# A three-stage transformer layer on one core: the twice folded filter's common part in three pieces from the sixth phase on, early weight transfers held back, first norms in another order

## The chip, the cores and the metric

The kernel runs on one core of a Trainium2 chip. The core has a matrix engine (PE; its weight loads are listed apart as PEld), a vector engine (DVE), a scalar or activation engine (ACT), a general engine (POOL) and a queue engine (SP) that issues most DMAs. The metric is the device time of one launch in microseconds (us). Smaller is better.

## The reference

The input is a 2 x 1024 x 512 float32 tensor. Four blocks follow each other, each a residual on the normalised input: differential attention with a filter along the tokens, a mixture of 8 experts of which 2 are kept, a linear attention with rotary embedding, and the same mixture again. The change touches the first block only:

```python
q, k, v = (norm(x) @ W for W in (Wq, Wk, Wv))      # 16 heads, two halves of 16 each
q, k = rotary(q), rotary(k)                        # interleaved pairs
attn1, attn2 = causal(q1, k1, v), causal(q2, k2, v)
f = rfft(attn1, axis=1) - lambda_full * rfft(attn2, axis=1)
attn = irfft(f * exp(-0.5 * (linspace(0, 1, n) / 0.15) ** 2), n=1024, axis=1)
attn = attn * rsqrt(mean(attn * attn, -1) + eps) * rms_weight * (1 - LAMBDA_INIT)
x = x + attn.reshape(2, 1024, 512) @ Wout
```

The filter in frequency is a circular convolution along the 1024 tokens. The kernel does it with 128 x 128 blocks of taps.

## The kernel before

**Opening.** The first batch's eight tiles of 128 tokens are loaded in the order 4, 5, 6, 7, 0, 1, 2, 3 and normalised in pairs. `pair_sums` (DVE statistics, then two ACT functions for the inverse root) and `pair_scale` (three small DVE operations, then two 128x512 scalings, line 125) are called for one pair after another, each pair's sums ahead of the scaling of the pair before. `spread` turns a tile with four PE transposes (L313) and one ACT copy (L316). `project` makes 256 tokens of queries and keys of a unit with four matmuls that the trace counts as eight (L344); piece k-1 is called after the tiles of pair k are turned, and the last piece at the end. `project_values` (L368) makes the values. `rotate` multiplies the raw result and a copy of it with neighbouring rows exchanged (`other`, a DMA on SP, L360) by two tables and adds them (L388 to L390; DVE for unit 0, POOL for the others). It then sends parts to `keys` (L392, SP) and, once per unit, to `swapped` (L397: two DMAs from `qk`, two from `keys`). For unit 0 all four of those last DMAs are issued by ACT, for the other units by SP.

**Transfers.** DMAs on SP wait for each other only by place in the queue, by the data they need and by their buffers. A load of weights into a tile that nothing has used yet needs nothing. `load_others` brings the first expert weight `wdr`, `wup` and the filter's taps `filt`; `load_weights` and `load_values` bring 256 KB of attention weights for each later unit or pair of units.

**The attention loop.** There are 16 units (batch, quarter of the heads, half of a quarter) of nine phases. The loop counts steps t = 9 x unit + phase, from 0 to 143, and six more steps that drain it. One step makes the scores of two row blocks (L464, L477, PE), finds their minima (L491, L499, DVE), exponentiates (L508, ACT), joins the two halves of the step before (L543, DVE, with ratios from POOL, L528 and L536), transposes the joined weights of the step before that (L567, PE, and L569, ACT), and takes in whatever the dictionaries `small`, `large`, `middle`, `final` and `rear` list for that step. `large` entries share one PSUM bank per step while their widths add up to 512. `weigh` (L594) and `finish` (L616) turn weights into results at steps 9u+6, 9u+7, 9u+11 and 9u+13 (12 for the last two units). `fold` adds and subtracts rows of the result on POOL. PE, DVE, ACT and POOL keep the order in which the program calls; SP's order comes from a scheduler.

**Mixing.** The first four tiles of the second block's input (`MIXED`) are filtered inside the last two units, where unit 15 has no next unit to project. With t0 = 126 the first step of unit 14:

- `mix_common` (four matmuls of 256 columns, which the trace counts as eight, L719; an ACT copy, L728) at t0+5 for one half of the columns and t0+8 for the other; `mix_part` 0 and 1 (two POOL operations of 128x256 each, L748) one step later.
- `mix_apart` (four matmuls of 512 columns, L734; copy L739) at t0+9 and t0+10; `mix_part` 2 and 3 (two POOL operations of 128x512, L751 and L752) one step later.
- per tile n: `mix_square` (POOL, L756) at t0+10+n, `mix_sum` (DVE, L760) one step later, `mix_tables` (ACT) and `mix_scale` (three small DVE operations, then POOL, L771) after that; `mix_turn` (four transposes, L777, and a copy, L780) and `mix_project` (four matmuls of 512 columns, L786, and a DVE addition, L788) at t0+14, +17, +18 and +19, that is at steps 140, 143, 144 and 145. Steps from 144 on have no scores any more.
- POOL scales one quarter of `wout` (L851) in each of the steps 135 to 138.

The lines that set these places:

```python
            FILTER = [5, 8, 9, 10]
            TURN = [14, 17, 18, 19]
            t = (NU - 2) * NP
            for k, f in enumerate(FILTER):
                at(large, t + f, mix_common if k < 2 else mix_apart, 512, k % 2)
                at(middle, t + f + 1, mix_part, k)
```

## Time and profile before

| | |
|---|---|
| times of three runs | 1159.13, 1153.18 and 1149.43 us; median 1153.18 us |
| the profiled execution's own time | 1153.29 us |
| its span, first to last instruction | 1151.4 us, mean granted clock 0.988 |
| busy: ACT / POOL | 766.7 us (67%) / 437.8 us (38%) |
| first scores against `keys` (L477) | 38.02 us |
| steps 109 to 117 (unit 12, nothing mixed) | 40.28 us |
| steps 127 to 135 (unit 14) | 42.97 us |
| steps 136 to 143, to the last L534 | 47.75 us |
| from there to the end of the span | 439 us |

The steps are measured from one reciprocal of the join (L534, one in each step from 1 to 144) to the next. PE's work of a step starts up to 1 us ahead of that step's reciprocal. A row of the timeline gives start, duration, engine, line, operation, tiles and count, and in brackets how long the engine sat idle before and what released it. A row of the busy time by stretch gives the stretch, its length, the busy time of PE, PEld, DVE, ACT and POOL, the granted clock of the matrix engine, and the DMA share and rate.

### The profile page before, as it was taken

What the parts mean: (1) busy time and instruction counts of PE and PEld (TensorE: products, weight loads), DVE (VectorE), ACT (ScalarE), POOL (GpSimd) and SP (SyncE); (2) the same over time, 40 slices, a digit from 0 to 9 for tenths busy, and PEclk for the clock granted to TensorE, in tenths of its full rate; (3) what the DMA queues carried; (4) which work ended last, traced back from release to release, by engine and by line L of the source; (5) the groups of instructions that cost most, each with busy time, mean ns of one, the idle gap of its engine ahead of it and who ended that gap; (6) DMA issues with size and microseconds to landing.
All of it is one profiled execution on the core that took longest, in us unless ns stands there. A gap on an engine that the chain in (4) does not pass through costs nothing.

```text
span 1151.4 us, 23472 instructions
## 1 busy us (share of the span) xinstructions
PE 1068.3 (93%) x8680; PEld 732.3 (64%) x8680; DVE 930.3 (81%) x2034; ACT 766.7 (67%) x2009; POOL 437.8 (38%) x689
## 2 busy tenths in 40 slices
PE   6799999999889999999999888889999999998997
PEld 5677777777677787777777655545555544454554
DVE  5599999999889889989998987577777777757576
ACT  3488988989989889999989876243434333342533
POOL 0245456445354544634544562123232222223200
PEclk9999999999999999999999989899999999999999
DMA  5412211201301101110110611200000000000002
GB/s 194 156 47 66 59 35 57 61 27 45 116 16 38 45 17 36 46 43 15 39 43 20 235 55 39 110 1 1 1 1 1 1 1 0 1 1 37 1 19 92
DMA packets 33345, 52.19 MB, mean 45 GB/s; under 512 B 6480, under 2 KB 11088, under 8 KB 33104
## 3 DMA queue, kind: packets, MB, share of 16 engines
q1 hardware_dynamic: 32912, 50.17, 13.6%
q8 instruction: 69, 1.13, 0.4%
q10 hardware_dynamic: 320, 0.52, 0.2%
q14 instruction: 44, 0.36, 0.1%
HBM read 23.42 MB, written 6.29 MB: 26 GB/s over the span
## 4 chain that ended last, share of the span: by engine, by line
PE 54%; DVE 25%; ACT 12%; issue 5%; POOL 2%; DMA 2%; SPq 0%; DVEq 0%; POOLq 0%; ACTq 0%
DVE least L499 9%; ACT p L508 8%; PE s L477 7%; DVE p L543 6%; PE py L1269 4%; PE pq_q L1206 4%; PE pq_v L1206 4%; PE bank L344 4%; PE pq_k L1206 4%; PE dtp L567 4%; PE z L1010 3%; PE bank L594 3%; DVE least L491 3%; PE hr_f L1074 3%; PE po_f L1144 3%
## 5 line engine op out<-in xcount | busy, mean ns | idle before, releaser
L508 ACT ACTIVATE p<-s,least 128x640 f32<-128x640 f32 (+7 forms) x512 | 378.2, 744 | 47.5 <-DVE least L499 28.1
L499 DVE TENSOR_REDUCE least<-s 128x1 f32<-128x896 f32 (+5 forms) x384 | 244.2, 679 | 35.2 <-PE s L477 35.2
L543 DVE SCALAR_TENSOR_TENSOR p<-p,ratio,p 128x1024 f32<-128x1024 f32 (+7 forms) x256 | 226.7, 921 | 3.6 <-POOL ratio L536 3.4
L567 PE MATMUL dtp<-ident,p 128*128 128x128 f32 x1152 | 184.1, 283 | 11.8 <-ACT dt L569 7.6
L569 ACT COPY dt<-dtp 128x512 f32<-128x512 f32 x288 | 168.8, 586 | 38.7 <-PE dtp L567 35.2
L477 PE MATMUL s<-keys,qk 32*128 32x128 f32 (+3 forms) x1408 | 168.4, 442 | 3.1 <-DMA keys<-qk 3.1
L567 PEld LDWEIGHTS dtp<-ident,p 128*128 128x128 f32 x1152 | 128.1, 141 | 56.4 <-ACT dt L569 31.3
L491 DVE TENSOR_REDUCE least<-s 128x1 f32<-128x1024 f32 (+1 forms) x96 | 115.9, 1213 | 26.4 <-PE s L477 26.4
L477 PEld LDWEIGHTS s<-keys,qk 32*128 32x128 f32 x1408 | 94.2, 187 | 56.0 <-issue 49.6
L536 POOL TENSOR_TENSOR ratio<-ratio,inverse 128x2 f32<-128x2 f32 (+1 forms) x144 | 28.1, 195 | 243.2 <-DVE inverse L534 220.2
L528 POOL TENSOR_TENSOR ratio<-sums,neg_lam 128x2 f32<-128x2 f32 (+1 forms) x144 | 74.5, 517 | 118.8 <-ACT p L508 118.7
L344 PE MATMUL bank<-xnT,wqk 128*128 128x256 f32 x472 | 116.0, 389 | 2.6 <-ACT raw L355 1.7
L477 PE MATMUL s<-swapped 32*128 32x128 f32 (+2 forms) x896 | 105.4, 347 | 0.0
L508 ACT ACTIVATION_READ_ACCUMULATOR p<-s,least 128x1 f32 x512 | 104.0, 203 | 0.0
L344 PEld LDWEIGHTS bank<-xnT,wqk 128*128 128x128 f32 x472 | 85.7, 191 | 18.0 <-ACT raw L355 5.5
L464 PE MATMUL s<-eye 128*128 128x256 bf16 (+1 forms) x320 | 61.6, 251 | 20.6 <-ACT p L508 19.3
L477 PEld LDWEIGHTS s<-swapped 32*128 32x128 f32 x896 | 71.9, 187 | 9.3
L594 PE MATMUL bank<-dt,v 128*32 128x128 f32 x2304 | 69.5, 274 | 1.6 <-ACT v L376 0.5
L594 PEld LDWEIGHTS bank<-dt,v 128*32 128x32 f32 x2304 | 60.9, 110 | 8.5 <-ACT v L376 4.3
L389 POOL TENSOR_TENSOR other<-other,rope_a_sb 128x512 f32<-128x512 f32 x30 | 63.0, 2099 | 0.0
L1229 POOL TENSOR_TENSOR qkv_v<-qkv_v,qkv_k 128x512 f32<-128x512 f32 x16 | 20.4, 1273 | 109.3 <-DVE qkv_v L1228 108.2
L368 PE MATMUL bank<-wval,xnT 128*128 128x128 f32 x448 | 60.5, 283 | 0.9
(217 smaller groups left out, 1789.8 us busy)
## 6 DMA issues: line engine op xcount, KB each, us to landing
other<-raw SPq DMA_DIRECT2D x64, 128.0 KB, 2.1
xin<-in_query SPq DMA_DIRECT2D x16, 256.0 KB, 3.0
keys<-qk SPq DMA_DIRECT2D x64, 64.0 KB, 1.9
x_sb<-in_query SPq DMA_DIRECT2D x16, 256.0 KB, 6.0
out_dram<-x_sb SPq DMA_DIRECT2D x16, 256.0 KB, 2.2
swapped<-qk SPq DMA_DIRECT2D x30, 128.0 KB, 2.3
swapped<-keys SPq DMA_DIRECT2D x30, 128.0 KB, 2.3
wqk<-in_w_qk SPq DMA_DIRECT2D x8, 256.0 KB, 4.8
```

The source lines that it names most:

```text
L344: nc.tensor.matmul(pp, wqk[:, part, c, :], xnT[b, half][:, c, t0 : t0 + 256], start=(c == 0), stop=(c == EC - 1),)
L389: engine.tensor_mul(other, other, rope_a[:, 1, cols])
L477: nc.tensor.matmul(s[mm][:, c0 : c0 + w], q[r0 : r0 + 32, j * P - back : (j + 1) * P - back], k[r0 : r0 + 32, s0 - back : s0 - back + w], ...
L491: nc.vector.tensor_reduce(least[n][:, e[0] : e[-1] + 1 : e[-1] - e[0] or 1, mm], s[mm].rearrange("p (g k) -> p g k", g=g), AX.X, ALU.min,)
L499: nc.vector.tensor_reduce(least[n][:, e, mm : mm + 1], s[mm][:, c0 : c0 + w], AX.X, ALU.min)
L508: nc.scalar.activation(ps[mm][:, c0 : c0 + w], sv, AF.Exp, bias=low, scale=-1.0, accum_out=sums[n][mm][:, e : e + 1],)
L528: nc.gpsimd.tensor_mul(ratio[:, w], first, neg_lam.to_broadcast([P, w.stop]))
L543: nc.vector.scalar_tensor_tensor(ps[0][:, c0 : c0 + w], ps[1][:, c0 : c0 + w], ratio[:, k : k + 1], ps[0][:, c0 : c0 + w], ALU.mult, ALU.add,)
L567: nc.tensor.transpose(tp[:, k * P : (k + 1) * P], d[:, c0 : c0 + P], ident)
L569: nc.scalar.copy(dt[:, 4 * half : 4 * half + 4, :], tp.rearrange("p (k q) -> p k q", k=4))
L594: nc.tensor.matmul(po[32 * g : 32 * g + 32, c0 : c0 + P], vals[n // 2 % 2][:, k, 64 * (n % 2) + 32 * h : 64 * (n % 2) + 32 * h + 32], dt[: ...
L1206: nc.tensor.matmul(pq, hTs[n][:, c, :], win(c, s), start=(c == 0), stop=(c == EC - 1))
```

## The change

Five things are changed.

1. `stay` writes one column of a tile with zeros on DVE. The loads of `wqk` for units 2 to 7, of `wval` for pairs 1 to 3, and of `wdr`, `wup` and `filt` now come after such a write in the same call, so that the DMA waits for DVE to get there.
2. `wdr` and `wup` with `filt` are called at steps 20 and 22, not 2 and 4.
3. For unit 0 the two `swapped` DMAs that read `keys` are issued by SP, those that read `qk` by ACT as before.
4. The second half of the common filter part is split in two entries of 256 columns at t0+6 and t0+7 (they share banks with `weigh` and `finish` of unit 14). Everything behind it comes one step sooner: `mix_apart` at t0+8 and t0+9, the squares from t0+9, the turns at t0+13, +14, +17 and +18, that is at steps 139, 140, 143 and 144.
5. In the opening, a pair is scaled before the next pair's sums are formed (for the first pair), the sums run one pair further ahead, and projection piece k follows directly on the turning of pair k.

In the order that the changed program has on SP, the opening's queue reads: eight tiles, tables, first weights, `wrms`, one tile, `other` (first half), one tile, `keys` (first half), `other` (second half), `swapped` from `keys`, `keys` (second half), `wval`. On ACT the two functions for the second pair come ahead of the first pair's two copies out of PSUM.

```diff
+            def stay(tile):
+
+                nc.vector.memset(tile[:, 0:1], 0.0)
+
             def load_weights(u):
+                if u > 1:
+                    stay(wqk[:, u, 0, :])
                 nc.sync.dma_start(wqk[:, u, :, :], i["w_qk"][u].rearrange("p (c f) -> p c f", c=EC))
 
             def load_values(pair):
+                if pair:
+                    stay(wval[:, pair, 0, :])
                 nc.sync.dma_start(wval[:, pair, :, :], i["w_val"][pair].rearrange("p (c f) -> p c f", c=EC))
...
                 elif k == 1:
+                    stay(wdr[:, 0, :])
                     nc.sync.dma_start(wdr, i["w_dr"].rearrange("(c p) f -> p c f", p=P))
                 elif k == 2:
+                    stay(wup)
+                    stay(filt[:, 0, :])
                     nc.sync.dma_start(wup, i["w_up"])
...
-                queue = nc.sync if u else nc.scalar
+                queues = nc.sync if u else nc.scalar, nc.sync
...
-                            queue.dma_start(
+                            queues[s].dma_start(
...
             for k in range(4):
-                at(rear, 2 * k, load_others, k)
+                at(rear, 2 * k + (18 if 0 < k < 3 else 0), load_others, k)
...
-            def mix_common(bank, c0, half):
+            def mix_common(bank, c0, half, ds):
                 cols = slice(256 * half, 256 * half + 256)
-                y = bank[:, c0 : c0 + 512]
-                for d in range(2):
+                y = bank[:, c0 : c0 + 256 * len(ds)]
+                for at_d, d in enumerate(ds):
                     products = sum_products(0, d)
...
-                sd = mix["sd"] = work.tile([P, 2, 256], F32, tag="sq", name=f"sd_{half}", bufs=3)
-                nc.scalar.copy(sd, y.rearrange("p (d f) -> p d f", d=2))
+                if ds[0] == 0:
+                    mix["sd"] = work.tile([P, 2, 256], F32, tag="sq", name=f"sd_{half}", bufs=3)
+                nc.scalar.copy(mix["sd"][:, ds[0] : ds[-1] + 1, :], y.rearrange("p (d f) -> p d f", d=len(ds)))
...
-            FILTER = [5, 8, 9, 10]
-            TURN = [14, 17, 18, 19]
+            FILTER = 8
+            TURN = [13, 14, 17, 18]
             t = (NU - 2) * NP
-            for k, f in enumerate(FILTER):
-                at(large, t + f, mix_common if k < 2 else mix_apart, 512, k % 2)
-                at(middle, t + f + 1, mix_part, k)
+            at(large, t + 5, mix_common, 512, 0, (0, 1))
+            at(middle, t + 6, mix_part, 0)
+            at(large, t + 6, mix_common, 256, 1, (0,))
+            at(large, t + 7, mix_common, 256, 1, (1,))
+            at(middle, t + 8, mix_part, 1)
+            for d in range(2):
+                at(large, t + FILTER + d, mix_apart, 512, d)
+                at(middle, t + FILTER + d + 1, mix_part, 2 + d)
             for n in range(MIXED):
-                f = t + FILTER[2] + 1 + n
+                f = t + FILTER + 1 + n
...
                 pair_sums(pairs[0])
                 for k, g in enumerate(pairs):
-                    if k + 1 < len(pairs):
-                        pair_sums(pairs[k + 1])
                     pair_scale(g)
+                    if k == 0:
+                        pair_sums(pairs[1])
                     for j in range(2):
                         finished(spread(2 * g + j, spare))
-                    if k:
-                        finished(project(spare(f"qk_{k}"), 0, 0, k - 1))
-                finished(project(spare("qk_4"), 0, 0, 3))
+                    if k + 2 < len(pairs):
+                        pair_sums(pairs[k + 2])
+                    finished(project(spare(f"qk_{k}"), 0, 0, k))
```

More of the change, by code (lines that the diff above doesn't have):

```diff
@@ L719, in mix_common @@
                         nc.tensor.matmul(
-                            y[:, 256 * d : 256 * d + 256],
+                            y[:, 256 * at_d : 256 * at_d + 256],
                             filt[:, tap, :],
```

## The prediction

> **What bounds the kernel now.** The page comes first, for the shares of the whole.

> ```profile
> PE 1068.3 (93%) x8680; PEld 732.3 (64%) x8680; DVE 930.3 (81%) x2034; ACT 766.7 (67%) x2009; POOL 437.8 (38%) x689
> PE 54%; DVE 25%; ACT 12%; issue 5%; POOL 2%; DMA 2%; SPq 0%; DVEq 0%; POOLq 0%; ACTq 0%
> ```

> PE and DVE take turns at holding the chain, and DMA has 2% of it, 23 us. The change touches two stretches only, the opening and the steps 131 to 146, so the timeline of the opening is next.

> ```profile
> 14.74 3.62 PE L344 MATMUL qk<-xnT,wqk 128*128 128x256 f32 x8
> ...
> 19.46 1.89 PE L344 MATMUL qk<-xnT,wqk 128*128 128x256 f32 x8
> ...
> 23.63 0.44 SPq L227 DMA_DIRECT2D wdr_sb<-in_w_dr  x1
> 24.12 0.50 SPq L229 DMA_DIRECT2D wup_sb<-in_w_up  x1
> 24.67 0.43 SPq L230 DMA_DIRECT2D filt_sb<-in_c_filt  x1
> 26.12 1.11 SPq L360 DMA_DIRECT2D other<-raw  x2
> ...
> 32.38 0.69 DVE L388 TENSOR_TENSOR raw<-raw,rope_a_sb 128x512 f32<-128x512 f32 x1 [5.83 <-DMA other<-raw]
> 32.88 1.12 ACTq L397 DMA_DIRECT2D swapped<-keys  x2
> 34.04 0.65 ACT L376 COPY v<-values 128x256 f32<-128x256 f32 x2 [4.38 <-DMA swapped<-qk]
> ...
> 38.02 0.70 PE L477 MATMUL s<-keys,qk 32*128 32x512 f32 x2 [3.06 <-DMA keys<-qk]
> 39.10 3.41 PE L344 MATMUL bank<-xnT,wqk 128*128 128x256 f32 x8
> ```

> The second exchanged copy (L360) is issued at 26.12 behind `wdr`, `wup` and `filt` and lands at 32.38, 6.3 us later; the first took 2.74 us (issued 21.79, used by DVE at 24.53). Rotation, `keys` and the first scores at 38.02 hang on it. The eight matmuls of one projection take 3.62 us early and 1.89 later, and 3.41 again after PE's wait. The busy time by stretch shows why:

> ```profile
> 34.90:38.00 3.10, 0.06 (x1) 0.01 (x1) 0.00 (x0) 0.12 (x1) 0.00 (x0) 1.00 0.74 221
> ...
> 39.50:43.00 3.50, 3.50 (x14) 2.47 (x16) 2.09 (x2) 2.51 (x5) 0.19 (x1) 0.51 0.78 263
> ```

> PE idles for 3 us and is then granted half its clock for 3.4 us. Last, the steps of the mixing:

> ```profile
> 649.00:654.00 5.00, 3.76 (x33) 2.91 (x34) 4.28 (x10) 3.87 (x11) 1.81 (x7) 1.00 1.03 389
> 654.00:658.10 4.10, 3.62 (x28) 2.63 (x27) 3.74 (x7) 4.03 (x11) 1.92 (x3) 1.00 1.04 383
> 658.10:664.40 6.30, 6.30 (x32) 3.44 (x32) 4.61 (x6) 4.21 (x8) 3.70 (x5) 1.00 1.04 403
> ...
> 683.00:688.90 5.90, 4.18 (x31) 3.44 (x31) 5.80 (x14) 4.58 (x13) 3.24 (x4) 0.71 0.00 0
> 688.90:697.40 8.50, 8.47 (x103) 5.26 (x102) 6.91 (x21) 4.61 (x15) 1.40 (x3) 1.00 0.01 2
> ...
> 717.20:722.40 5.20, 4.96 (x24) 2.46 (x26) 0.64 (x1) 1.67 (x3) 0.00 (x0) 1.00 0.00 0
> ```

> These are steps 133, 134, 135, 139, 140 and 145. Step 135 holds `mix_apart` and is all PE, step 140 a turn and projection and all PE, step 139 is held by DVE, step 145 has nothing but PE's turn and projection.

> **The opening, part by part.** *Order of the norms.* The two ACT functions of the first pair end at 5.97; with the second pair's sums out of the way, three small DVE operations (0.58 in all, 8.22 to 8.80) and two scalings (1.00) end at 7.6 instead of 9.8. PE turns the pair (1.94, L313) by 9.1. ACT now does the second pair's functions first: two statistics of 0.69 and two of 0.18, three casts (0.47) and one addition (0.17) put their start at 10.0 and their end at 10.45; two copies of 0.59 then end at 11.65, and projection 0 starts there, not at 14.95. From here I follow PE. Projection 0 still slow, 3.62: 15.3. Eight transposes between the two rates, 1.47: 16.8, and a copy, 0.6, that PE must now wait for: 17.4. Projection 1 at 1.89: 19.3. Then transposes 1.04, copy 0.6, projection 1.89, twice: 26.4, against 25.7 now. So the order begins 3.3 us earlier and loses all of it to three exposed copies. Values 7.31 and the next unit's first piece 1.89: 35.6, scores at 35.9.

> *Held transfers.* The second exchanged copy is issued at 26.8 with nothing ahead of it in transfer: 2.74 to landing, 29.5; L388 to L390, 2.0; `keys` issued at 31.7, landing by 35.0 even at the 3.4 us that it took under load. The DMA chain, now last by far, is then 0.9 us ahead of PE. `swapped` from `keys` on SP is issued between, at 28, and frees ACT of the 4.38 us wait; SP's `keys` of the second half stands behind it, but needs DVE until 31.6. First scores: 38.02 to 35.9, 2.1 saved. Bounds: nothing, if PE is slow until projection 1 ends, to 3.0, if it is fast from the middle of projection 0.

> *Half clock.* With PE busy up to the scores, L344 at 39.10 takes 1.9, not 3.41. The next scores (42.65) need the first exponential as well, which ended at 41.60; they could start 0.2 later, so 0.85 is saved, not 1.5. Bounds 0 and 1.5.

> [...]

> *The zero writes.* Twelve on DVE, of one column; nearest rows POOL's memset of that shape (0.10), a 128x2 operation on DVE (0.15 to 0.17) and 0.07 between two starts of such. 12 x 0.07 to 0.17 is 0.8 to 2.0 us. They stand after a join and ahead of the next minima, where DVE waits for the scores in 89 of 144 steps (61.6 us in all): that hides most of it. I take +0.4, range 0 to 2.0.

> *What the held loads queue behind.* On SP the next DMA is ready later than the write in every case I traced: at step 4 the write falls at 61 (the next step's L534 less its first minima) and `keys` is issued at 67.7, at step 13 at 102.9 and 103.9, at step 18 at 126.8 and 127.1. At step 18 a 256 KB load (4.8 us from issue to landing) stands ahead of a copy which POOL uses at 133.0: 127.1 + 0.5 + 4.8 is 132.4, so still in time. What POOL then makes is used at step 27, 37 us later. `wdr`, `wup` and `filt` are first needed at step 131 or later. Nothing, as long as that cover holds.

> **The mixing.** Per step, from PE's busy time: a common half costs 1.96, an apart part 3.6, a turn with projection 0.7 in the step before and 3.7 in its own.
> - 132: +1.0 of PE on 3.97 in a step of 4.40: +0.6.
> - 133: PE 3.76 loses 0.8 and gains 1.8, in a step of 5.00 which waits for POOL's ratio: 0.
> - 134: 3.62 - 1.2 + 2.8 = 5.2 against 4.10: +1.1.
> - 135: 6.30 less 0.5 of PE: -0.5. `mix_part` 2 and a square fall here, POOL 6.1: it just fits.
> - 136: PE 5.90 loses 3.0; DVE, with a sum of 0.83 more and slowed joins, takes over at 5.5: -0.4. 137 stays (6.00, now as 5.85).
> - 138: one sum's contention less, but a turn begins: -0.3.
> - 139: PE 4.18 - 0.7 + 3.7 + 0.7 = 7.9, less what of it was inflated by half clock (0.4): +1.6. 140 unchanged, the first turn replaced by the second.
> - 142: no scaling behind the ratios: -0.4.
> - 145: the turn and projection of 722.40 are gone; PE needs the two transposes (0.66 each) and the copy between (0.59) before `weigh`, which starts at 719.0 instead of 722.35: -3.3.

> Sum -1.6. Bounds: the refunds of 135 to 142 missing and 0.6 less in the tail, +0.6; the additions hidden, -4.5.

> **Sum.** -2.1 - 0.85 + 0.4 - 1.6 = -4.2, against the profiled execution's own 1153.29 (span 1151.4 and 1.9 around it): **1149.1 us**. The median of the runs is 0.1 less than that execution, so no shift. The three runs shown differ by 9.7 us, so about 1% is what a measurement here can tell from no change.

> **The rivals.**
> - *PE replaces the DMA in the opening* (0.14). The exposed copies and a late clock leave the scores at 38.0; the half clock alone is saved. 1153.3 - 0.85 + 0.4 - 1.6 = 1151.2. For it: my PE chain is only 2.1 ahead. Against: the same PE work, begun 3.3 earlier.
> - *The mixing gains nothing* (0.17). Steps 132, 134 and 139 pay in full and 135 to 142 give nothing back, since DVE was the next there (5.85 of 6.00, 5.80 of 5.90): +0.6 for that part, 1151.3. For it: the DVE column. Against: step 145, which has no other work.
> - *Alternation keeps the clock low* (0.09; slower). Projections of 3.6 us now stand between transposes and waits. If PE gets its clock only among the values, projections 1 to 3 cost 1.73 more each, three groups of transposes 0.93 more (0.43 of it is counted) and the first values 1.7: scores at 45, 1153.3 + 7.1 - 0.85 + 0.4 - 1.6 = 1158.3. It decides for slower once scores start after 40.1. For it: now, too, full rate came only after 14.74 to 18.4, a whole projection without a break. Against: at 684.6 to 688.1 a stretch made up of transposes and scores at 0.51 was followed by 1.00.

> [...]

> - *Held loads hold up the rotation* (0.06; slower). If the nine 256 KB loads land after POOL is due, POOL's in-order queue stalls (its one such wait now is 2.5 us) and the join's ratio behind it: 9 x 2.5 on 1149.1 is 1171. It decides where a landing takes over 5.4 us.
> - *Both ends gain their bounds* (0.10): -3.0 - 1.5 - 4.5 is 1144.3; 1141 and less needs the loop to gain as well, which no row shows.

> That the change does not do what it says is excluded for the transfers: in the changed program each such DMA waits for DVE.

> **The numbers.** The forecast has 0.44. It and the first two rivals lie between 1146 and 1152.5. The range 1143.5 to 1156 takes in the fifth and the upper bounds of the unknown costs (2.0 for the writes, 2.2 for the mixing over the forecast), and leaves out the slow clock and the stalled rotation, 0.15. Faster than 1141.6: half of the fifth rival, 0.05. Slower than 1164.7: the stalled rotation and the far end of the slow clock, 0.07. Within 1%: 0.88.

> **What would show it.** Right: first scores near 36 with no DMA wait in front of them, L344 behind them at 1.9, the second L360 landing within 3 us, units 0 to 5 as long as now, step 134 and 139 longer by 1 to 2 us, and `weigh` of the drain 3 us closer to the last reciprocal. Wrong: a wait of DVE or PE for a DMA among the steps 0 to 60, a granted clock of half in steps 137 to 140, or L344 at 3.6 beyond 18 us.

## The result, and the profile after

| | before | after |
|---|---|---|
| median of the runs | 1154.15 us (14 runs, 1149.43 to 1159.13) | 1146.82 us (14 runs, 1145.01 to 1148.91) |
| the profiled execution, its span | 1153.29, 1151.4 us | 1146.25, 1144.1 us |

The ratio is 0.9937 with a 95% interval of 0.9923 to 0.9952: 7.3 us less, by the interval 5.5 to 8.9. That is inside the forecast range and within 1%; the forecast gain was 4.2.

Line numbers are now those of the kernel after: L355 is the old L344, L488 the old L477, L371 the old L360. First two lines of its page, the busy time and the chain by engine:

```profile
PE 1066.4 (93%) x8680; PEld 730.9 (64%) x8680; DVE 929.6 (81%) x2046; ACT 765.9 (67%) x2010; POOL 437.9 (38%) x689
PE 56%; DVE 24%; ACT 12%; issue 5%; POOL 1%; DMA 1%; DVEq 0%; SPq 0%; ACTq 0%; POOLq 0%
```

No engine does noticeably less; DMA's share of the chain went from 2% to 1%. The opening on PE (start, duration, engine, line; in brackets the idle time before and what ended it):

```profile
11.04 3.78 PE L355 MATMUL qk<-xnT,wqk 128*128 128x256 f32 x8 [1.94 <-ACT xnT L327]
...
16.62 1.99 PE L355 MATMUL qk<-xnT,wqk 128*128 128x256 f32 x8 [0.73 <-ACT xnT L327]
...
20.21 1.99 PE L355 MATMUL qk<-xnT,wqk 128*128 128x256 f32 x8 [0.73 <-ACT xnT L327]
...
23.81 1.99 PE L355 MATMUL qk<-xnT,wqk 128*128 128x256 f32 x8 [0.73 <-ACT xnT L327]
...
25.64 7.31 PE L379 MATMUL values<-wval,xnT 128*128 128x128 f32 x64
...
32.78 1.89 PE L355 MATMUL qk<-xnT,wqk 128*128 128x256 f32 x8
...
34.51 0.28 PE L475 MATMUL s<-eye 128*128 128x128 bf16 x2
...
34.72 0.70 PE L488 MATMUL s<-keys,qk 32*128 32x512 f32 x2
...
35.80 1.99 PE L355 MATMUL bank<-xnT,wqk 128*128 128x256 f32 x8
```

Projection 0 starts 3.7 us earlier than before (14.74), yet the values start at 25.64 against 25.52: three idle times of 0.73, each ended by ACT's copy, are what the forecast called exposed copies. The first scores stand at 34.72 with no wait in front of them (38.02, after 3.06 idle), and L355 behind them takes 1.99, not 3.41. The issue on SP of the second exchanged copy, and its first use by DVE:

```profile
26.24 1.97 SPq L371 DMA_DIRECT2D other<-raw  x2
...
29.82 0.69 DVE L399 TENSOR_TENSOR raw<-raw,rope_a_sb 128x512 f32<-128x512 f32 x1 [5.99 <-ACT v L387]
```

3.6 us lie between issue and use, where 6.3 lay before. (The row names ACT's copy of `v` as what ended DVE's wait; L399 reads nothing of it, and it ended at about the same time as the transfer.) Then busy time by stretch (stretch, length, busy time and count of PE, PEld, DVE, ACT and POOL, granted clock, DMA share, GB/s), for steps 134, 139, 140, 143 and 145:

```profile
649.70:655.70 6.00, 5.95 (x31) 3.22 (x30) 4.69 (x6) 4.39 (x11) 3.84 (x5) 1.00 1.05 382
679.50:688.30 8.80, 7.83 (x46) 4.61 (x45) 7.00 (x21) 4.96 (x15) 1.39 (x3) 0.93 0.01 2
688.30:693.90 5.60, 5.60 (x58) 3.12 (x60) 4.87 (x12) 4.18 (x12) 1.39 (x3) 1.00 0.00 0
703.20:708.90 5.70, 5.70 (x23) 3.38 (x22) 3.15 (x6) 4.38 (x12) 0.39 (x2) 0.88 0.57 184
714.30:719.00 4.70, 3.51 (x87) 2.88 (x87) 0.17 (x2) 1.60 (x4) 0.00 (x0) 1.00 0.12 17
```

Steps 139 and 140 have changed places (5.90 and 8.50 before), with DVE's 21 instructions moved along with the long one. The trace grants half the clock from 673.87 to 680.69, which is step 138 and the start of 139, and from 701.17 to 704.59, which is the end of step 142 and the start of 143. The last stretch has no turn and projection any more: 80 of its 87 small matmuls are already `weigh`. Step lengths, from one reciprocal of line 534 (545 after) to the next, counted from the first instruction on an engine (0.24 us into the span) to the last one (3.24 us before its end, before and after; the last output transfer follows):

| stretch | before | after | difference | forecast |
|---|---|---|---|---|
| to the reciprocal of step 1 | 44.90 | 40.73 | -4.17 | -2.95 |
| steps 1 to 126 | 576.31 | 576.34 | +0.03 | +0.4 |
| steps 127 to 143 | 90.72 | 91.65 | +0.93 | +1.7 |
| from the last reciprocal to the last instruction on an engine (the tail) | 435.98 | 431.93 | -4.05 | -3.3 |
| sum | 1147.91 | 1140.65 | -7.26 | -4.2 |

### The profile page after: what moved, and what is told of

It reads as the page before. It is cut to its first block, busy times and chain, and to the rows that moved or that the text cites. A ratio compares the mean times of both kernels' runs of the same rounds, so it can differ in the third digit from the quotient of the medians.

```text
span 1144.1 us, 23492 instructions
## 1 busy us (share of the span) xinstructions
PE 1066.4 (93%) x8680; PEld 730.9 (64%) x8680; DVE 929.6 (81%) x2046; ACT 765.9 (67%) x2010; POOL 437.9 (38%) x689
## 4 chain that ended last, share of the span: by engine, by line
PE 56%; DVE 24%; ACT 12%; issue 5%; POOL 1%; DMA 1%; DVEq 0%; SPq 0%; ACTq 0%; POOLq 0%
DVE least L510 9%; ACT p L519 8%; PE s L488 8%; DVE p L554 6%; PE py L1287 5%; PE pq_q L1224 5%; PE pq_v L1224 4%; PE dtp L578 4%; PE pq_k L1224 4%; PE bank L355 4%; PE z L1028 3%; PE bank L605 3%; DVE least L502 3%; PE hr_f L1092 3%; PE po_f L1162 3%
## 5 line engine op out<-in xcount | busy, mean ns | idle before, releaser
L488 PE MATMUL s<-keys,qk 32*128 32x128 f32 (+3 forms) x1408 | 167.8, 441 | 0.0
L488 PEld LDWEIGHTS s<-keys,qk 32*128 32x128 f32 x1408 | 93.5, 186 | 49.9 <-issue 43.4
L355 PE MATMUL bank<-xnT,wqk 128*128 128x256 f32 x472 | 114.6, 386 | 2.8 <-ACT raw L366 1.8
L488 PE MATMUL s<-swapped 32*128 32x128 f32 (+2 forms) x896 | 104.8, 345 | 0.0
L355 PEld LDWEIGHTS bank<-xnT,wqk 128*128 128x128 f32 x472 | 85.0, 190 | 17.8 <-ACT raw L366 5.9
L475 PE MATMUL s<-eye 128*128 128x256 bf16 (+1 forms) x320 | 61.2, 251 | 17.3 <-ACT p L519 16.2
L488 PEld LDWEIGHTS s<-swapped 32*128 32x128 f32 x896 | 71.2, 185 | 9.4
```

Source lines behind the costliest of these rows:

```text
L355: nc.tensor.matmul(pp, wqk[:, part, c, :], xnT[b, half][:, c, t0 : t0 + 256], start=(c == 0), stop=(c == EC - 1),)
L488: nc.tensor.matmul(s[mm][:, c0 : c0 + w], q[r0 : r0 + 32, j * P - back : (j + 1) * P - back], k[r0 : r0 + 32, s0 - back : s0 - back + w], ...
```

## The experiments

The theory behind them, A: holding the loads back carries the whole gain of the opening, the new order of the norms carries none, and the mixing gains about 3 us in its tail. Rivals: the order is needed for it (B); the writes or the held loads cost something in the loop (C). Every run was timed against the kernel before on the same chip; the difference is the ratio's distance from 1 times 1154.

| run | its time, before beside it (us) | ratio, 95% | difference (us) |
|---|---|---|---|
| e1_order | 1155.78, 1154.63 | 1.0007, 0.9994 to 1.0021 | +0.8 |
| e2_hold | 1148.14, 1154.63 | 0.9948, 0.9932 to 0.9964 | -6.0 |
| e3_mix | 1151.57, 1154.63 | 0.9973, 0.9957 to 0.9989 | -3.1 |
| e4_no_order | 1145.12, 1154.63 | 0.9928, 0.9910 to 0.9946 | -8.3 |
| after_again | 1146.35, 1153.18 | 0.9945, 0.9923 to 0.9966 | -6.3 |
| h3_three | 1150.00, 1153.18 | 0.9972, 0.9960 to 0.9984 | -3.2 |
| t_old | 1149.66, 1153.18 | 0.9967, 0.9956 to 0.9979 | -3.8 |
| w1_warm | 1145.69, 1153.18 | 0.9926, 0.9902 to 0.9950 | -8.5 |
| f_fill | 1142.02, 1152.92 | 0.9905, 0.9886 to 0.9924 | -11.0 |
| wf_warm_fill | 1141.65, 1152.92 | 0.9909, 0.9886 to 0.9931 | -10.5 |
| g_drain | 1143.93, 1156.21 | 0.9899, 0.9881 to 0.9917 | -11.7 |
| gw_all | 1143.34, 1156.21 | 0.9892, 0.9873 to 0.9912 | -12.5 |

### One part at a time

**The order alone (e1_order).**

```diff
 for k, g in enumerate(pairs):
-    if k + 1 < len(pairs):
-        pair_sums(pairs[k + 1])
     pair_scale(g)
+    if k == 0:
+        pair_sums(pairs[1])
     for j in range(2):
         finished(spread(2 * g + j, spare))
-    if k:
-        finished(project(spare(f"qk_{k}"), 0, 0, k - 1))
-finished(project(spare("qk_4"), 0, 0, 3))
+    if k + 2 < len(pairs):
+        pair_sums(pairs[k + 2])
+    finished(project(spare(f"qk_{k}"), 0, 0, k))
```

> The kernel before with the new order of the norms alone; the second exchanged copy still stands behind the three weight loads. Theory A (the held loads carry the gain of the opening; the order only shifts the projections and loses the shift to three exposed copies): first scores 38.0, as before, because the copy lands at 32.4 as before; time 0 to 0.5 us less than before, 1153.5 to 1154.2. Rival B (the earlier start of PE is what counts, through an earlier full clock): first scores at 36 or earlier, 2 us or more saved.

First scores came at 38.07, after an idle time of 2.79 that a transfer of `keys` ended. There is no gain: B falls.

**The held loads alone (e2_hold).** The twelve writes and the two load groups called at steps 20 and 22, which is 18 steps later (the expectation says 9), without the rest. All four `swapped` DMAs of unit 0 stay on ACT here.

> The kernel before with the zero writes and the two load groups put 9 steps later alone. Theory A: the second exchanged copy lands in 2.7 us instead of 6.3, PE's own chain of norms, projections, values and one further piece becomes the bound, first scores 34.6 to 35.0, no half clock behind them; 4 us less than before, some 1150. Rival B: without the new order PE reaches its scores only at 36 or later; 1.5 to 2.5 us less. Rival C (writes and held loads cost something in the loop): steps 1 to 127 longer by 2 us or more than the 576.3 of before.

First scores came at 33.69, with no half clock behind them; the reciprocal of step 1 is 5.2 us earlier than before, 1.0 more than in the whole change. Steps 1 to 126 took 576.11. A's mechanism holds, and more was gained than it said (6.0 us for 4, scores 0.9 ahead of its range); C falls. The `swapped` DMAs that the change moves to SP are not needed for this; that part was never tried alone.

**The mixing alone (e3_mix).**

```diff
-FILTER = [5, 8, 9, 10]
-TURN = [14, 17, 18, 19]
+FILTER = 8
+TURN = [13, 14, 17, 18]
...
-for k, f in enumerate(FILTER):
-    at(large, t + f, mix_common if k < 2 else mix_apart, 512, k % 2)
-    at(middle, t + f + 1, mix_part, k)
+at(large, t + 5, mix_common, 512, 0, (0, 1))
+at(middle, t + 6, mix_part, 0)
+at(large, t + 6, mix_common, 256, 1, (0,))
+at(large, t + 7, mix_common, 256, 1, (1,))
...
```

> The kernel before with the new plan of the mixing alone (common part in three pieces, apart parts and turns a step earlier). Theory A: opening as before (first scores 38.0); steps 127 to 144 longer by 0.9, the stretch behind the last reciprocal shorter by 4.0: 3.1 us less than before, 1151. Rival (part of the tail's gain comes from the opening's shift against the clock's grid): less than 2 us saved, or a half clock in the tail.

The time fell as expected. The steps from 127 on took 90.96, 0.24 longer than before, and the tail 431.63, 4.35 shorter. The opening still had its idle time (3.23 before the first scores). Steps 1 to 126 took 579.13 here and 578.90 in e1_order, 2.8 and 2.6 longer than before though neither has a write; both traces have half clocks in steps 2, 3, 61 and 62, to which the last section comes back.

**All but the order (e4_no_order).** The changed kernel with the old lines of the first diff.

> The changed kernel with the old order of the norms put back. Theory A: first scores 34.6 to 35.0, the time within 0.5 us of the changed kernel (1146.8). Rival B: first scores 1.5 us or more later than the 34.72 of the changed kernel, 1148.5 or more.

First scores came at 33.27, 1.45 us earlier than in the changed kernel and ahead of what A said, and the time is not longer. The order is not merely without effect; it seems to cost about 1 us. To see whether that is only chance, the moment at which PE is done with all that stands ahead of the scores (the first L475), beside the moment at which the trace grants full clock:

| | full clock from | PE done |
|---|---|---|
| old order: before, e3_mix, e2_hold, e4_no_order | 19.03, 16.22, 16.72, 17.08 | 34.47, 32.99, 33.49, 33.06 |
| old order: t_old, h3_three, f_fill, g_drain | 18.28, 18.67, 15.40, 16.12 | 33.84, 34.13, 32.45, 32.95 |
| new order: after, after_again, e1_order | 15.10, 13.93, 16.50 | 34.51, 33.94, 35.00 |

With the new order the clock comes earlier by about 2 us, and PE is done 1.1 us later in the mean (34.48 against 33.42): the earlier start is more than spent on three bare copies.

### On one chip: the order again, the writes, the turns, the clock

**The changed kernel once more (after_again).**

> The changed kernel itself once more, for a comparison on one chip with the three kernels beside it, which all have the old order of the norms. Theory A (the new order costs about 1 us once the transfers are held: three copies of 0.73 stand bare on PE's path): ratio to before near 0.994, first scores between 34.5 and 35.0, 1 us above the kernel with three writes. Rival (the 1 us between the profiles is the clock's phase, which differs from execution to execution): within 0.5 us of it.

The ratio is as the first time; first scores came at 34.15, 0.57 earlier than in the first profile, with full clock 1.17 earlier. But the kernel it was to be compared with, h3_three, did not do what was expected of it, so the comparison by time fails: the cost of the order rests on the table above, and by time alone (e4_no_order and the two runs of the changed kernel have overlapping intervals) it is not settled. The three parts run alone add up to -8.3 us; the whole change measured -7.3 and -6.3, and the intervals cover the difference.

**Three writes of twelve (h3_three).**

```diff
 def load_weights(u):
-    if u > 1:
-        stay(wqk[:, u, 0, :])
...
 def load_values(pair):
-    if pair:
-        stay(wval[:, pair, 0, :])
```

> The changed kernel with the old order of the norms, and of the twelve zero writes only the three for wdr, wup and filt; the nine ahead of the loads of later units and pairs are left out. Theory A (only those three transfers stand in the way of the second exchanged copy): first scores 33.2 to 33.8, 1145.1 as with all twelve. Rival C (the nine writes or the loads they hold cost something): 0.5 us or more less. Rival D (the other loads stand in the way as well): second exchanged copy later than 3 us, first scores beyond 35.

This is rival D. The issues of SP in the opening, DVE's use of the second copy, and the first scores:

```profile
23.37 0.45 SPq L203 DMA_DIRECT2D wqk<-in_w_qk  x1
...
24.34 0.43 SPq L203 DMA_DIRECT2D wqk<-in_w_qk  x1
...
25.86 1.11 SPq L367 DMA_DIRECT2D other<-raw  x2
...
28.29 1.28 SPq L206 DMA_DIRECT2D wval<-in_w_val  x1
...
29.62 1.19 SPq L203 DMA_DIRECT2D wqk<-in_w_qk  x2
...
30.92 0.69 DVE L395 TENSOR_TENSOR raw<-raw,rope_a_sb 128x512 f32<-128x512 f32 x1 [4.64 <-DMA other<-raw]
...
32.97 1.17 SPq L399 DMA_DIRECT2D keys<-qk  x2
...
38.10 0.70 PE L484 MATMUL s<-keys,qk 32*128 32x512 f32 x2 [3.69 <-DMA keys<-qk]
```

With `wdr`, `wup` and `filt` out of the way, the loads of the later units run ahead into their place: two stand before the copy, three before the last `keys`, which take 5.1 us from issue to the scores. So the nine writes ahead of loads that nothing needs soon are needed as well; what they do without the other three was not tried.

**The old turns (t_old).** `TURN = [14, 17, 18, 19]` with everything else of e4_no_order.

> The changed kernel with the old order of the norms and the old steps of the four turns (14, 17, 18, 19), the common part still in three pieces. Theory A (the turn moved out of the last step carries the tail, and the move of the first expert norm the lengthening of step 139): the stretch behind the last reciprocal 436.0 again instead of 431.9, steps 139 and 140 at 5.9 and 8.5 again, steps 127 to 144 no longer than 91.5; 1149 in all. Rival (the earlier parts themselves carry part of it): tail at 434 or less, 1147 or less.

The tail is 435.10, 3.2 longer than with the new turns (431.89; 435.3 to 436.0 in before, e1_order and e2_hold), and steps 139 and 140 are 5.36 and 8.94: the long step is the one in which the first tile of x is finished and normalised, and it moves with the first turn. The sum of the two is 14.30; before it was 14.43, after 14.37. Steps 132 to 138 take 39.1 with either set of turns (before 38.4): that is the price of the earlier parts, +0.7.

**Early clock (w1_warm).**

```diff
+warm = spare("warm")
+for k in range(34):
+    nc.tensor.transpose(warm[:, k % 4 * P : k % 4 * P + P], ident, ident)
 pair_sums(pairs[0])
```

> The changed kernel with the old order of the norms and 34 extra transposes of the identity on PE ahead of the first norm, from 1.5 us on; they compute nothing that is used. Theory A (PE's chain sets the first scores and its clock, which came full only at 15.1 to 17.1, costs 1.7 of it; transposes alone bring it): clock full by 8.7, first transposes 1.04 instead of 1.94, projection 0 in 1.9 instead of 3.5, first scores 31.3 to 31.8; 1.7 us below the kernel with three writes, 1143.4. Rival E (transposes do not count as work for the clock): clock full only after projection 0, nothing gained. Rival F (the transfers of keys are next, at most 0.4 behind PE now): first scores at 32.8, 0.5 gained.

Two stretches of 3.41 us in the opening, then the two that lead into step 3:

```profile
3.93:7.34 3.41, 3.41 (x18) 3.41 (x17) 2.99 (x8) 0.41 (x2) 0.00 (x0) 1.00 1.00 314
7.34:10.75 3.41, 2.00 (x16) 1.49 (x14) 3.23 (x14) 1.48 (x4) 0.00 (x0) 1.00 1.04 356
...
41.48:44.89 3.41, 1.84 (x19) 1.17 (x19) 3.41 (x6) 2.88 (x7) 2.09 (x3) 1.00 0.00 0
44.89:48.30 3.41, 3.41 (x22) 2.92 (x15) 3.34 (x8) 2.30 (x7) 3.18 (x4) 0.50 0.00 0
```

The clock's record starts only with its first change (7.34, to full), so the 1.00 of the first row says nothing; in it 18 transposes fill 3.41 us, 0.19 each, and behind it the eight of the first pair took 1.11 us (1.94 in e4_no_order). Rival E falls: only transposes had run on PE until then, and without them (e4_no_order) full clock came from 17.08. First scores came at 32.20. The opening gained 1.1 us over e4_no_order, but PE waits for DVE there (2.55 before the second pair), and the time is no better: step 3 fell into half clock (5.01 for 4.31), and so did steps 60 to 62 (unit 6 took 43.05, 41.44 in e4_no_order). In each case PE had been busy for 0.54 of the 3.41 us before (1.84 of them ahead of step 3).

### Keeping the clock

**Work for idle places (f_fill).** The kernel of e4_no_order, and:

```diff
+def keep_busy(bank, c0):
+    for _ in range(5):
+        nc.tensor.transpose(bank[:, c0 : c0 + P], ident, ident)
+    yield
...
+for t in (2, 58, 59, 60, 61, 137, 138, 141, 142):
+    at(large, t, keep_busy, P)
```

> The changed kernel with the old order of the norms, and five extra transposes of the identity (0.65 us, into the free columns of the step's bank, used by nobody) between the two halves of PE's transposes in the steps 2, 58 to 61, 137, 138, 141 and 142. Theory A (in nine of ten traces the granted clock halves only after a stretch of 3.41 us in which PE was busy for 0.67 of it or less, in the tenth after 0.54, and transposes count as busy): no half clock in steps 2 to 4, 59 to 62 and 142 to 143; unit 6 at 41.2 whatever the phase, step 143 at 4.7 instead of 5.7; 1 us less than without, 1144. Rival (the added transposes stand on the path): these steps each 0.3 to 0.6 longer, 1148.

(The expectation gives the shares loosely; the last section has those of before and after.) From 15.40 to 718.54 the trace shows no half clock. Step 139 takes 7.74 where the changed kernel took 8.74, step 143 4.77 for 5.75; unit 6 stays at 41.64, so not all that was hoped for there. Its ratio ends at 0.9924, where the two intervals of the changed kernel begin (0.9923). The half clocks that are left lie behind the loop, the first of them here:

```profile
715.10:718.50 3.40, 1.21 (x7) 0.69 (x7) 2.21 (x5) 0.40 (x2) 1.97 (x6) 1.00 0.90 310
718.50:721.90 3.40, 1.93 (x9) 1.93 (x10) 1.27 (x4) 1.18 (x3) 1.05 (x3) 0.51 0.93 347
```

**Both (wf_warm_fill).**

> The same with the 34 early transposes ahead of the first norm as well. Theory A: clock full by 8.7, first scores 31.3 to 32.3, and no half clock in step 3 or steps 60 to 62, where the kernel with the early transposes alone lost 0.7 and 1.6; 2 to 3 us below the changed kernel, 1143 to 1144. Rival: what the opening gains comes back as waits of PE in the loop, 1145.7 as with the early transposes alone.

This is a miss for the early transposes. Two stretches of 3.41 us behind them:

```profile
10.14:13.55 3.41, 0.85 (x8) 0.60 (x7) 3.24 (x14) 1.35 (x4) 0.00 (x0) 1.00 1.01 367
13.55:16.96 3.41, 3.41 (x12) 2.88 (x12) 3.05 (x12) 1.29 (x3) 0.00 (x0) 0.50 0.40 100
```

The clock came at 6.73 and was half again from 13.55, behind a stretch in which PE had 0.85 us of work and waited for DVE: projection 0 took 3.23, the first scores came at 33.34, 0.52 later than in f_fill. There was no half clock in the loop, but the stretch behind the last reciprocal took 434.01, 1.85 more than in f_fill.

**The drain (g_drain).** Added to f_fill, ahead of three groups of transposes that wait:

```diff
 tp = ps_t.tile([P, 512], F32, tag="tp", name=f"tp_{key}")
+for _ in range({"f0_0": 10, "f0_1": 14, "y4": 14}.get(key, 0)):
+    nc.tensor.transpose(tp[:, 0:P], ident, ident)
```

> The kernel with the old order of the norms and the nine groups of five extra transposes, and 10, 14 and 14 more transposes of the identity (into the bank that the next real transposes overwrite) where PE waits in the drain for the first two scaled tiles and for the fifth mixed tile. Theory A (a stretch with PE busy for less than half of it brings 3.4 us at half clock, also in the drain): no half clock at 718 to 725 and at 742; the 16 matmuls of L1100 there take 2.0 instead of 3.8; 2 to 3 us below the kernel with the nine groups alone (1142), 1139.5. Rival (the chain there runs through DVE and ACT): no half clock, but less than 0.7 gained.

The gain over f_fill (0.7 by the ratios) is the rival's, for other reasons. In this execution the first scores came at 34.56, 1.7 later than in f_fill, after PE had waited 1.33 for a transfer of `keys`: the transfers are close behind PE in the opening (t_old and f_fill wait 0.23 and 0.09 for them), and here they came last. The tail took 431.97, 0.2 less than f_fill's 432.16:

```profile
721.70 2.03 PE L1102 MATMUL hr_f<-wdr_sb,xT_f 128*128 128x136 f32 x16
...
741.79 1.99 PE L966 MATMUL tp_y<-ident 128*128 128x128 f32 x14 [2.68 <-ACT hT_b L1215]
...
743.57 1.06 PE L968 MATMUL tp_y<-ident,yn 128*128 128x128 f32 x4
```

The first two groups did their work (2.03 for 3.83). The third had to wait for its bank, which ACT frees at 741.79, so its 14 transposes came after the idle time instead of in it, and put the real ones 1.8 us back; a half clock from 743.16 to 746.57 remained.

**All (gw_all).** g_drain with the 34 early transposes and 14 more ahead of the second pair's.

> The same with 34 early transposes and 14 more ahead of the second pair's, where PE waits 2.55 for DVE. Theory A: clock full before 8.7 and not halved again at 13.6 as in the run with the early ones alone; first scores 31.7 to 32.3, 0.6 to 1.5 before the 32.8 of the kernel with the nine groups; 1138.5. Rival (the first scores are set by DVE's norms and by the transfers, not by the clock): first scores at 32.8 or later, nothing gained over the kernel beside it.

The clock was full from 6.07 to 739.93 without a break. First scores came at 32.66, just 0.16 before f_fill's. That is the rival, since PE waits for DVE's norms and for ACT's copies there. The tail was 430.19. The ratio, 0.9892 (0.9873 to 0.9912), lies wholly below that of the changed kernel, but not clear of f_fill's.

## Why the prediction was right, and where its terms were off

- **Order of the norms.** Right, and a little kind: the earlier start (3.7 us, forecast 3.3) is lost to the copies. Over the traces PE is done 1.1 us later with the new order; the times neither confirm nor refute it.
- **Held transfers, first scores -2.1: the size was off; measured -3.3.** The mechanism was as told (PE, not the transfer, sets the scores). The chain of PE was to reach the scores at 35.9 and reached them at 34.72. Of the 1.2 us, 0.6 is that projection 0 started at 11.04 and not at 11.65, because ACT had its functions and copies done sooner; 0.3 is that the values and the further piece took 8.9 from start to end, not 9.2; the rest is in small pieces, among them eight transposes counted at the rate between (1.47) that took 1.27. The copies cost more than forecast, 0.73 for 0.6. The second exchanged copy, 3.6 us from issue to use for a forecast of 2.74, was too slow for the sum but still off the path.
- **What holds them.** The step named `wdr`, `wup` and `filt` as what stood before the second copy, and the other nine writes only as a cost. h3_three shows that the device does not work without them: 3.2 of e4_no_order's 8.3 us are left, which is what the mixing brings alone. This was a gap in the reasoning that the result hid.
- **Half clock, -0.85.** Right: step 1's reciprocal gained 4.17, 0.87 beyond the scores (granted clock 1.00 from 34.51 to 38.60).
- **Zero writes, +0.4.** Nothing: the steps 1 to 126 differ by 0.03. Each of the twelve writes took 0.06. The reason given, that DVE waits there, fits only three of them (0.69 to 1.52 of idle time behind them); the others start within the recorded time of the operation ahead of them, and DVE goes on without a pause. **Held loads in the queue, 0:** right.
- **Mixing, the steps: +1.7, measured +0.93.** 132 (+0.52), 133 (-0.55), 135 (-0.37), 136 (-0.46), 137 (-0.20), 138 (-0.05) and 142 (-0.76) came out within 0.6 of their terms; 134 cost 1.83 for 1.1. The step that failed is "139: +1.6, 140 unchanged"; they measured +2.85 and -2.91. The forecast counted PE's work of the turn and left out DVE's first expert norm, which follows the first finished tile and moves with it. In step 139 of the changed kernel the norm starts with

```profile
683.84 0.69 DVE L800 TENSOR_TENSOR x_sb<-x_sb,bank 128x512 f32<-128x512 f32 x1 [1.12 <-PE bank L798]
...
685.04 0.69 DVE L968 BATCH_NORM_STATS2 bn_f<-x_sb 128x6 f32<-128x512 f32 x1
```

  and its last small operation ends at 687.18; only behind it does DVE form the next minima, from scores that PE began at 683.95, and the next reciprocal stands at 688.29. Of the 2.85, 1.0 is the half clock up to 680.69: in e3_mix and the last four runs, with full clock there, step 139 took 7.73 to 7.74. Step 143, not forecast, cost another 1.0 through a half clock. So it is partly luck that the sum came near +1.7: two half clocks made up for most of what step 140 gave back.
- **Mixing, the tail: -3.3, measured -4.05.** Mechanism right: `weigh` starts 6.36 us after the last reciprocal, 10.18 before. The term was made from 719.0 as its start and was 0.5 short; the remaining 0.2 lies behind it.
- **The rivals.** "PE replaces the DMA" came true as a mechanism, but not at its price, since PE's chain was 3.3 ahead and not 0. The slow clock (alternation) did not: full clock came earlier with the new order, not later (15.10 in the changed kernel, 19.03 before), and in w1_warm it came at 7.34 with nothing but transposes on PE until then. The fifth case (1144.3) was 2.5 from the result, the forecast 2.3; its bound of -4.5 for the mixing is -4.9 by the terms themselves, with the additions of 132, 134 and 139 left out.
- **The signs.** One sign of being wrong came: a granted clock of half in steps 138 and 139. It could not tell, since the kernel before has it there too (677.80 to 681.22 and 684.63 to 688.04). Step 139 also grew by more than the 1 to 2 us named as a sign of being right.

Of the total, first scores (1.2), tail (0.75), steps of the mixing (0.8) and writes (0.4) each came out better than forecast; all four errors have the same sign, so they add up to 3.1.

## What to carry to other kernels

Holding back one load does little while the next, which waits for nothing either, may take its place: in h3_three loads of later units were issued at 23.37 and 24.34, ahead of the second exchanged copy at 25.86. Hold back all that a short chain of transfers must not meet (three of the twelve writes alone left the first scores at 38.10, all twelve brought them to 33.27). Starting an engine earlier was worth nothing where the new order put every copy between two of its pieces (projection 0 began 3.7 us earlier, and PE was done at 34.51, 34.47 before); compare the time at which it is done, not the time at which it starts. And before a percent is looked for in an order, look at the stretches at half clock: five transposes at idle times in nine steps of the loop took 1.9 us off the span in one execution of each kernel (2.7 by the ratios, whose intervals overlap), where the change as a whole took 7.3.
